# A four-layer graph network: layer 2's edge sums by bitwise and of two 8-bit adjacencies in place of matmuls in layer 1

## The chip, the cores and the metric

The kernel runs on one NeuronCore of a Trainium2 chip. The metric is the device time of one execution in microseconds (us); the number compared is the median of several runs. A profile is one further execution, recorded by the hardware profiler; its own time and the median of the other runs are not the same number, and both are given below.

## The reference, cut to what matters

There are N = 4096 nodes with D = 256 features, and one symmetric 0/1 adjacency `adj` (4096 x 4096, fp32) with ones on its diagonal. Four graph layers follow one another; each ends with `x = layernorm(x + layer(x, adj))`.

```python
# layer 0: mean over neighbours, concat, linear, relu
agg = adj @ x / max(deg, 1);  relu(concat([x, agg]) @ W + b)
# layer 1, two steps: R is adj + I with rows normed; A is a softmax attention cut to its top 0.9 of mass
A = top_p(softmax(q @ k.T));  Xf = R @ Xf;  Xa = A @ Xa;  Z += Xf @ U1.T + Xa @ U2.T
# layer 2, called with edge_features = adj
nn = adj @ x
ne = einsum('ij,ji->i', adj, edge_features)      # one number for each row
concat([x, nn, ne]) @ weight + bias
# layer 3: symmetric normed adjacency, linear, relu
```

The change is about `ne`: for row i it is the sum over j of `adj[i, j] * adj[j, i]`, a count of edges that exist both ways.

## The kernel before

**Tiling.** P = 128, so there are NT = 32 blocks of 128 rows. The host hands the adjacency over in two orders, both fp32 in DRAM: `adjt[it]`, the transposed blocks of block row `it` (a partition is a column, the layout that a matmul takes as its stationary side), and `adjn[it]`, the blocks of the other orientation. The main products run over a block row: 32 stationary tiles of 128x128 (fp32r, cast by ScalarE from 8-bit copies) against a moving 128x512 tile that holds the upper and the lower half of the features' bits side by side.

**Layer 0** (lines 220 to 349). `l0_main` loads `adjt[it]` in two halves by a DMA that casts fp32 to 8-bit (L276, on GpSimd's queue, 1 MB of source each) into a slot of the tag `in` (nine slots, eight of which first hold the input features), stores the 8-bit copy to `adj8_d[it]` in DRAM (L277, on SyncE's queue), and multiplies it. `column_counts` (L287) sums a block row's bits on VectorE: a tree of uint16 adds (L292, L294, L299), one shift (L296) and a cast (L301); one matmul with a column of ones (L306) ends the sum. The shift and the factor PER_ONE = 7 come from the bit pattern of an 8-bit 1.0. `l0_end` uses a layer norm whose reciprocal root is a GpSimd instruction (L197), and stores x1 and x1 + ln_b (L331, L332).

**Layer 1** (lines 352 to 1096) has two steps, n = 0 and 1. For each block i, `pieces` (L720) goes over eight chunks g of 512 columns; a chunk holds logits of block i+2 (L411), the attention product of block i, and `neighbours` (L674), which is R's product of block i+2 (acc_r, L683, with L685 for the identity). In step 0 the attention product is sparse: sixteen rows of x1 per node are fetched by indirect DMAs on GpSimd's queue (`gather`, L669, eight buffers; fetch k+8 follows the matmul of k) and multiplied by diagonal tiles (L758). In step 1 it is dense (turns L741, matmuls L766). VectorE finds the maxima and the kept ones (L430, L527, L660). `flag` (L579) counts by two fp32 matmuls (L589, L590) how many rows have to be put off to a later pass, and scatters their numbers (L603, GpSimd's queue).

In step 0 only, `neighbours` also makes `ne`: it loads `adjn[i]` in two halves by a casting DMA (L689, GpSimd's queue, into two slots of the step's pool) and multiplies each 8-bit tile of the one orientation by that of the other into one PSUM bank, tag `nef` (L693, 32 matmuls of 128x128 a block); `r_end` takes the diagonal of the result (L707) into column i of the tile `nef`. As `nef` is taken, acc_r has only the bank `acc` in step 0 (`r_acc`, L696, `nef_done`); later it has both in turn.

**Layers 2 and 3** (lines 1101 to 1184). `piece` loads a quarter of a block row of `adj8_d` (SyncE's queue, L1104, five slots) and casts it (ScalarE, L1106, four slots); `main` multiplies it. `l2_end` adds the residual and the parts (L1134, L1135 on VectorE, `nef` at L1137), and `l2_y` makes the operand of layer 3, for which layer 3 waits.

**What sets the order.** The kernel is written in a framework that builds all data dependencies and waits itself. It does not keep the program's order: at build time it plays the whole program against a list of costs, and gives each engine and each queue, at each moment, the earliest-written of the instructions whose data, buffers and engine are free. Each queue then runs in that fixed order on the chip; an instruction that waits holds up those behind it on its queue.

Names to keep: `ps_acc` is the PSUM pool with the two banks `acc` and `nef`; `half("mm")` and `half("acc")` are halves of two more banks; `hpool` holds the moving operand.

Of the kernel before, what the change touches and what calls it, by code (L numbers as in the profile page):

```python
# [24 lines left out]
P = 128  # L25
# [29 lines left out]
def gnn_stack(ctx, tc, x, adjt, adjn, w0, b0, w1, w2t, w3t, u1t, u2t, ln_g, ln_b, w2, b2, w3, b3, out):  # L55
# [44 lines left out]
    nc.vector.memset(ones_col, 1.0)  # L100
    mhalf = const.tile([P, 1], F32, name="mhalf")
# [18 lines left out]
    adj8_d = [dram.tile([P, NT, P], F8, name=f"adj8_{it}_d") for it in range(NT)]  # L120
    h_d = dram.tile([N + P, D], F32, name="h_d")
# [97 lines left out]

    with tc.tile_pool(name="l0", bufs=1) as l0, tc.tile_pool(name="l0w", bufs=2) as l0w:  # L220
# [28 lines left out]
        ones_bf = l0.tile([P, 1], BF16, name="ones_bf")  # L249
        nc.vector.memset(ones_bf, 1.0)  # L250
# [20 lines left out]
        def l0_main(it):  # L271
# [13 lines left out]
            return acc, column_counts(a8)  # L285

        def column_counts(a8):  # L287

            pairs = a8.bitcast(U16).rearrange("p j i -> p (j i)")
            W = NT * P // 4  # L290
            s = l0w.tile([P, W], U16, tag="sums", name="sums", bufs=1)
            nc.vector.tensor_add(s, pairs[:, :W], pairs[:, W:])  # L292
            W //= 2
            nc.vector.tensor_add(s[:, :W], s[:, :W], s[:, W : 2 * W])  # L294
            words = s[:, :W].bitcast(I32)
            nc.vector.tensor_scalar(words, words, 3, None, op0=ALU.logical_shift_right)  # L296
            while W > P // 2:
                W //= 2
                nc.vector.tensor_add(s[:, :W], s[:, :W], s[:, W : 2 * W])  # L299
            counts = l0w.tile([P, P], BF16, tag="counts", name="counts")  # L300
            nc.vector.tensor_copy(counts, s[:, :W].bitcast(U8))  # L301
            return counts
# [49 lines left out]
    with tc.tile_pool(name="l1", bufs=1, reuse_waits="tile") as l1:  # L352

        cur = {"late": False, "n": 0, "nef_done": False}
# [4 lines left out]
        ones_sq = l1.tile([P, P], F32, name="ones_sq")  # L359
        nc.vector.memset(ones_sq, 1.0)  # L360

        before = l1.tile([P, P], F32, name="before")
# [216 lines left out]
        def flag(st):  # L579
# [9 lines left out]
            nc.tensor.matmul(pb[:, 0:1], ones_sq, st["bad"], start=True, stop=True)  # L589
            nc.tensor.matmul(pb[:, 1:2], before, st["bad"], start=True, stop=True)  # L590
# [83 lines left out]
        def neighbours(n, i, g, acc_r, pn, xf):  # L674
# [11 lines left out]
            if pn is not None:  # L686
                if g % (NLC // 2) == 0:
                    cur["b8"] = cur["w"].tile([P, NT // 2, P], F8, tag="adjn8", name="adjn8", bufs=2)
                    nc.gpsimd.dma_start(cur["b8"], adjn[i, :, g * GP : g * GP + NT // 2, :])  # L689
                k = g % (NLC // 2) * GP  # L690
                for j in range(GP):
                    jt = g * GP + j
                    nc.tensor.matmul(pn[:, :P], cur["a8"][:, g % 2 * GP + j, :], cur["b8"][:, k + j, :], start=(jt == 0),  # L693
                                     stop=(jt == NT - 1))

        def r_acc(i):  # L696

            return ps_acc.tile([P, 512], F32, tag=("acc", "nef")[i % 2 if cur["nef_done"] else 0], name="acc_r", bufs=1)

        def r_end(i, acc_r, pn):  # L700
# [3 lines left out]
            if pn is not None:  # L704

                junk = spare_row.bitcast(F32)[:, :P]
                nc.vector.scalar_tensor_tensor(junk, pn[:, :P], 1.0, ident, op0=ALU.mult, op1=ALU.mult,  # L707
                                               accum_out=nef[:, i : i + 1])
            nc.sync.dma_start(rows(xf_d, i), xf_new)

        def r_product(n, i, xf):

            acc_r, pn = r_acc(i), None
            if n == 0:
                pn = ps_acc.tile([P, 512], F32, tag="nef", name="nef_ps", bufs=1)
            for g in range(NLC):
                neighbours(n, i, g, acc_r, pn, xf)
# [508 lines left out]
```

## Time and profile before

| | us |
|---|---|
| median of 3 runs | 3256.97 (3252.47 to 3258.52) |
| profiled execution, its own time | 3212.81 |
| its span, first to last instruction | 3211.1 |
| PE busy | 2949.0 (92%) |
| VectorE (DVE) busy | 2289.4 (71%) |
| ScalarE (ACT) busy | 1745.9 (54%) |
| GpSimd (POOL) busy | 786.8 (25%) |
| edge matmuls L693: first to last start | 359.9 to 1191.7 |
| R's product L683, both steps | 366.7 to 2468.1 |
| layer 2's matmuls | 2683.5 to 2960.8 |
| layer 3's matmuls | 2961.4 to 3197.1 |

How to read it: "busy" is the union of an engine's instructions. A busy PE is not PE at its peak, since matmuls are pipelined and each record reaches past the start of the next one: what a group of matmuls costs is read from its first start to the next group's start. The share of busy time is an average over stages with different limits; a stage has to be read from its own stretch. "DMA share" is the mean busy share of the core's sixteen DMA engines. A line such as "X L1 <- Y L2: total, times, longest" says that engine X sat idle before line L1 until line L2 on Y released it. PEld is the loading of stationary tiles, POOLq and SPq are the queues on which GpSimd and SyncE issue DMAs.

### The profile page before, as it was taken

What the parts mean: (1) busy time and instruction counts of PE and PEld (TensorE: products, weight loads), DVE (VectorE), ACT (ScalarE), POOL (GpSimd) and SP (SyncE); (2) the same over time, 40 slices, a digit from 0 to 9 for tenths busy, and PEclk for the clock granted to TensorE, in tenths of its full rate; (3) what the DMA queues carried; (4) which work ended last, traced back from release to release, by engine and by line L of the source; (5) the groups of instructions that cost most, each with busy time, mean ns of one, the idle gap of its engine ahead of it and who ended that gap; (6) DMA issues with size and microseconds to landing.
All of it is one profiled execution on the core that took longest, in us unless ns stands there. A gap on an engine that the chain in (4) does not pass through costs nothing. (4 is left out here: it accounts for less than half of the span.)

```text
span 3211.1 us, 45754 instructions
## 1 busy us (share of the span) xinstructions
PE 2949.0 (92%) x14376; PEld 2329.4 (73%) x14376; DVE 2289.4 (71%) x7161; ACT 1745.9 (54%) x2906; POOL 786.8 (25%) x915
## 2 busy tenths in 40 slices
PE   8999889999999996799989899989999796999998
PEld 3788667777777774578877777877788554887886
DVE  4666778888888875269979896988799664444444
ACT  3555655666666654365545454545555334666664
POOL 1121256677666763000000001000100100000000
PEclk9999999999999998899999999999999898999999
DMA  9995467777778774310001110111011234333332
GB/s 175 164 173 117 83 114 141 144 143 143 141 142 150 152 140 118 118 50 25 24 24 27 34 39 24 32 32 37 29 35 27 71 119 139 109 108 101 106 110 81
DMA packets 247872, 300.14 MB, mean 93 GB/s; under 512 B 34688, under 2 KB 201536, under 8 KB 247616
## 3 DMA queue, kind: packets, MB, share of 16 engines
q0 software_dynamic: 46576, 104.94, 22.9%
q1 hardware_dynamic: 188800, 180.93, 18.4%
q10 hardware_dynamic: 12240, 11.23, 1.1%
q8 instruction: 116, 1.90, 0.2%
q14 instruction: 140, 1.15, 0.2%
HBM read 331.17 MB, written 66.45 MB: 124 GB/s over the span
## 5 line engine op out<-in xcount | busy, mean ns | idle before, releaser
L683 PE MATMUL acc_r<-xh,adjq 128*128 128x512 f32 x2048 | 608.5, 428 | 27.7 <-ACT adjq L680 18.6
L766 PE MATMUL acc_bank<-xa,at 128*128 128x256 f32 x2304 | 565.6, 386 | 27.9 <-ACT at L744 27.3
L669 POOL DMA_INDIRECT G<-x_d,cols x512 | 496.1, 969 | 262.6 <-PE acc_bank L758 154.1
L680 ACT CAST adjq<-adj 128x512 fp32r<-128x512 fp8e4 x512 | 316.5, 620 | 386.5 <-PE acc_r L683 308.2
L766 PEld LDWEIGHTS acc_bank<-xa,at 128*128 128x128 f32 x2304 | 422.3, 193 | 88.2 <-ACT at L744 38.7
L683 PEld LDWEIGHTS acc_r<-xh,adjq 128*128 128x128 f32 x2048 | 376.0, 191 | 123.1 <-ACT adjq L680 45.4
L197 POOL TENSOR_TENSOR rstd<-ve,mhalf 128x1 f32<-128x1 f32 x168 | 103.1, 614 | 1337.8 <-DVE ve L195 1270.5
L430 DVE MAX8 cand<-e 128x8 f32<-128x256 f32 x1024 | 382.9, 415 | 65.0 <-ACT e L412 63.7
L412 ACT COPY e<-lg 128x512 f32<-128x512 f32 x552 | 319.5, 585 | 195.8 <-PE lg L411 191.9
L411 PE MATMUL lg<-kS,q 128*128 128x512 f32 x1104 | 398.2, 446 | 4.6 <-ACT e L412 4.5
L1106 ACT CAST a<-a 128x1024 fp32r<-128x1024 fp8e4 x256 | 267.9, 1048 | 156.7 <-PE acc L173 121.3
L758 PE MATMUL acc_bank<-G,dg 128*128 128x256 f32 x1024 | 288.5, 399 | 61.8 <-DMA G<-x_d,cols 48.2
L527 DVE FIND_INDEX8 cols<-top,e 128x8 uint32<-128x4096 f32 x64 | 282.8, 4419 | 0.0
L758 PEld LDWEIGHTS acc_bank<-G,dg 128*128 128x128 f32 x1024 | 195.1, 196 | 117.8 <-DMA G<-x_d,cols 65.9
L173 PE MATMUL acc<-xh,a 128*128 128x512 f32 x1024 | 255.0, 402 | 20.2 <-DMA a<-adj_d 15.5
L173 PE MATMUL acc<-y0h,a 128*128 128x512 f32 x1024 | 253.6, 401 | 0.0
L173 PEld LDWEIGHTS acc<-xh,a 128*128 128x128 f32 x1024 | 190.6, 189 | 63.8 <-ACT xh L149 23.0
L173 PE MATMUL acc<-yh,a 128*128 128x512 f32 x1024 | 233.7, 390 | 0.0
L744 ACT COPY at<-at_ps 128x512 f32<-128x512 f32 x296 | 173.5, 588 | 98.7 <-PE at_ps L741 97.0
L173 PEld LDWEIGHTS acc<-yh,a 128*128 128x128 f32 x1024 | 192.2, 188 | 39.6
L173 PEld LDWEIGHTS acc<-y0h,a 128*128 128x128 f32 x1024 | 188.1, 188 | 42.0 <-issue 0.6
L185 ACT COPY xt<-tr 128x256 f32<-128x256 f32 (+1 forms) x268 | 111.9, 425 | 189.8 <-PE tr L183 172.8
(287 smaller groups left out, 4588.0 us busy)
## 6 DMA issues: line engine op xcount, KB each, us to landing
adj<-adj_d SPq DMA_DIRECT2D x256, 128.0 KB
a<-adj_d SPq DMA_DIRECT2D x256, 128.0 KB
a<-in_adjt POOLq DMA_DIRECT2D x64, 256.0 KB
adj_d<-a SPq DMA_DIRECT2D x64, 256.0 KB
adjn<-in_adjn POOLq DMA_DIRECT2D x64, 256.0 KB
x_d<-x SPq DMA_DIRECT2D x64, 128.0 KB
xf_d<-xf_new SPq DMA_DIRECT2D x64, 128.0 KB
G<-x_d,cols POOLq DMA_INDIRECT x512
```

What stands on the lines that cost most here:

```text
L173: nc.tensor.matmul(acc, a[:, j, :], halves(jt), start=(jt == 0), stop=(jt == NT - 1))
L411: nc.tensor.matmul(pl[:, :LC], q[k], kS[:, s], start=(k == 0), stop=(k == 1))
L412: nc.scalar.copy(l[:, s], pl[:, :LC])
L430: nc.vector.max(dst[:, 8 * g : 8 * g + 8], src[:, g * GW : (g + 1) * GW])
L527: nc.vector.max_index(st["at"][:, 8 * r : 8 * r + 8], t8, st["e"][:, :N])
L669: nc.gpsimd.indirect_dma_start(out=g, out_offset=None, in_=x1_d, in_offset=bass.IndirectOffsetOnAxis(ap=st["at"][:, k : k + 1], axis=0))
L680: nc.scalar.copy(a, cur["a8"][:, g % 2 * GP : (g % 2 + 1) * GP, :])
L683: nc.tensor.matmul(acc_r, a[:, j, :], xf[:, jt, :], start=(jt == 0), stop=False)
L744: nc.scalar.copy(at[:, :G, :], ps[:, :G, :])
L758: nc.tensor.matmul(acc_a, dg[:, k % 4, :], st["G"][k], start=(k == 0), stop=(k == KEPT - 1))
L766: nc.tensor.matmul(acc_a, ats[g][:, j, :], cur["xa"][:, jt, :], start=(jt == 0), stop=(jt == NT - 1))
L1106: nc.scalar.copy(a, a8)
```

## The change

It makes a second 8-bit copy in DRAM, `adjn8_d`, by 64 DMAs that read `adjn` in fp32 and write 8 bits, written in the program at chunks 0 and 4 of each block of step 1. The edge matmuls, their loads and the diagonal leave step 0. In layer 2 each block loads its 512 KB row of `adjn8_d` (`edge_row`, two slots, SyncE's queue), VectorE takes the bitwise and with each of the four pieces (`both`), and `column_counts`, now with a pool as argument, sums the bits; `edge_count` ends the sum by a matmul and two small VectorE instructions. Beside that: acc_r uses both banks in step 0 too; `flag` casts `bad` to bf16 and takes bf16 matmuls; two adds of `l2_end` move to GpSimd; and the scratch of layer 2's first loads shares its slot with the second half of layer 3's operand.

```diff
@@ -98,6 +98,8 @@
     make_identity(nc, ident)
     ones_col = const.tile([P, 1], F32, name="ones_col")
     nc.vector.memset(ones_col, 1.0)
+    ones_bf = const.tile([P, 1], BF16, name="ones_bf")
+    nc.vector.memset(ones_bf, 1.0)
     mhalf = const.tile([P, 1], F32, name="mhalf")
     nc.vector.memset(mhalf, -0.5)
     rs = const.tile([P, NT], F32, name="rs")
@@ -118,6 +120,7 @@
     list_d = [dram.tile([N + P, 1], I32, name=f"list{n}_d") for n in range(STEPS)]
     adj8_d = [dram.tile([P, NT, P], F8, name=f"adj8_{it}_d") for it in range(NT)]
+    adjn8_d = [dram.tile([P, NT, P], F8, name=f"adjn8_{it}_d") for it in range(NT)]
     h_d = dram.tile([N + P, D], F32, name="h_d")
     k_d = dram.tile([N + P, P], F32, name="k_d")
@@ -215,6 +218,24 @@
         up = upper(ps[:, :P])
         nc.scalar.copy(dst[:DA, :], up[:DA, :])
         nc.vector.tensor_sub(dst[DA:, :], ps[DA:, :P], up[DA:, :])
+
+
+    def column_counts(pool, a8):
+
+        pairs = a8.bitcast(U16).rearrange("p j i -> p (j i)")
+        W = NT * P // 4
+        s = pool.tile([P, W], U16, tag="sums", name="sums", bufs=1)
+        nc.vector.tensor_add(s, pairs[:, :W], pairs[:, W:])
+        W //= 2
+        nc.vector.tensor_add(s[:, :W], s[:, :W], s[:, W : 2 * W])
+        words = s[:, :W].bitcast(I32)
+        nc.vector.tensor_scalar(words, words, 3, None, op0=ALU.logical_shift_right)
+        while W > P // 2:
+            W //= 2
+            nc.vector.tensor_add(s[:, :W], s[:, :W], s[:, W : 2 * W])
+        counts = pool.tile([P, P], BF16, tag="counts", name="counts", bufs=2)
+        nc.vector.tensor_copy(counts, s[:, :W].bitcast(U8))
+        return counts
     with tc.tile_pool(name="l0", bufs=1) as l0, tc.tile_pool(name="l0w", bufs=2) as l0w:
@@ -246,8 +267,6 @@
         x1 = xpool.tile([P, NT, D], F32, tag="X", name="x1")
         y0h = hpool.tile([P, NT, 2 * D], F32R, tag="H", name="y0h")
         deg1 = l0.tile([P, NT], F32, name="deg1")
-        ones_bf = l0.tile([P, 1], BF16, name="ones_bf")
-        nc.vector.memset(ones_bf, 1.0)
         def l0_weights(it, xt):
@@ -282,24 +301,7 @@
                 return a
             adj_matmul(l0w, acc, it, lambda jt: y0h[:, jt, :], piece)
-            return acc, column_counts(a8)
-
-        def column_counts(a8):
-
-            pairs = a8.bitcast(U16).rearrange("p j i -> p (j i)")
-            W = NT * P // 4
-            s = l0w.tile([P, W], U16, tag="sums", name="sums", bufs=1)
-            nc.vector.tensor_add(s, pairs[:, :W], pairs[:, W:])
-            W //= 2
-            nc.vector.tensor_add(s[:, :W], s[:, :W], s[:, W : 2 * W])
-            words = s[:, :W].bitcast(I32)
-            nc.vector.tensor_scalar(words, words, 3, None, op0=ALU.logical_shift_right)
-            while W > P // 2:
-                W //= 2
-                nc.vector.tensor_add(s[:, :W], s[:, :W], s[:, W : 2 * W])
-            counts = l0w.tile([P, P], BF16, tag="counts", name="counts")
-            nc.vector.tensor_copy(counts, s[:, :W].bitcast(U8))
-            return counts
+            return acc, column_counts(l0w, a8)
         def l0_degrees(it, counts):
             pd = half("acc")
@@ -351,15 +353,15 @@
     with tc.tile_pool(name="l1", bufs=1, reuse_waits="tile") as l1:
-        cur = {"late": False, "n": 0, "nef_done": False}
+        cur = {"late": False, "n": 0}
         FIRST = [[range(k * NT // 16, (k + 1) * NT // 16) for k in range(2)]]
         FIRST.append([range(5 * NT // 32, 8 * NT // 32), range(8 * NT // 32, 11 * NT // 32)])
-        ones_sq = l1.tile([P, P], F32, name="ones_sq")
+        ones_sq = l1.tile([P, P], BF16, name="ones_sq")
         nc.vector.memset(ones_sq, 1.0)
-        before = l1.tile([P, P], F32, name="before")
+        before = l1.tile([P, P], BF16, name="before")
         nc.gpsimd.affine_select(before, ones_sq, pattern=[[1, P]], compare_op=ALU.is_gt, fill=0.0, base=0,
                                 channel_multiplier=-1)
         ident_r = l1.tile([P, P], F32R, name="ident_r")
@@ -586,8 +588,10 @@
                 st["nb"] = small("nbad", 1, I32)[:1, :]
                 nc.scalar.copy(st["nb"], pb[:1, :1])
                 return
-            nc.tensor.matmul(pb[:, 0:1], ones_sq, st["bad"], start=True, stop=True)
-            nc.tensor.matmul(pb[:, 1:2], before, st["bad"], start=True, stop=True)
+            bad = small("bad16", 1, BF16)
+            nc.vector.tensor_copy(bad, st["bad"])
+            nc.tensor.matmul(pb[:, 0:1], ones_sq, bad, start=True, stop=True)
+            nc.tensor.matmul(pb[:, 1:2], before, bad, start=True, stop=True)
             sofar, slot = small("sofar"), small("slot")
             nc.vector.tensor_add(sofar, later["base"], pb[:, 0:1])
@@ -671,7 +675,7 @@
         GP = LC // P
-        def neighbours(n, i, g, acc_r, pn, xf):
+        def neighbours(n, i, g, acc_r, xf):
             if g % 2 == 0:
                 cur["a8"] = cur["w"].tile([P, 2 * GP, P], F8, tag="adj8", name="adj8", bufs=3)
@@ -683,39 +687,27 @@
                 nc.tensor.matmul(acc_r, a[:, j, :], xf[:, jt, :], start=(jt == 0), stop=False)
             if g + 1 == NLC:
                 nc.tensor.matmul(acc_r, ident_r, xf[:, i, :], start=False, stop=True)
-            if pn is not None:
-                if g % (NLC // 2) == 0:
-                    cur["b8"] = cur["w"].tile([P, NT // 2, P], F8, tag="adjn8", name="adjn8", bufs=2)
-                    nc.gpsimd.dma_start(cur["b8"], adjn[i, :, g * GP : g * GP + NT // 2, :])
-                k = g % (NLC // 2) * GP
-                for j in range(GP):
-                    jt = g * GP + j
-                    nc.tensor.matmul(pn[:, :P], cur["a8"][:, g % 2 * GP + j, :], cur["b8"][:, k + j, :], start=(jt == 0),
-                                     stop=(jt == NT - 1))
+        def second_copy(i, k):
+
+            half = slice(k * NT // 2, (k + 1) * NT // 2)
+            nc.gpsimd.dma_start(adjn8_d[i][:, half, :], adjn[i, :, half, :])
         def r_acc(i):
-            return ps_acc.tile([P, 512], F32, tag=("acc", "nef")[i % 2 if cur["nef_done"] else 0], name="acc_r", bufs=1)
-
-        def r_end(i, acc_r, pn):
+            return ps_acc.tile([P, 512], F32, tag=("acc", "nef")[i % 2], name="acc_r", bufs=1)
+
+        def r_end(i, acc_r):
             xf_new = work.tile([P, D], F32, tag="xf_new", name="xf_new", bufs=1)
             nc.scalar.activation(xf_new, acc_r[:, :D], AF.Copy, scale=rs[:, i : i + 1])
             nc.vector.scalar_tensor_tensor(xf_new, acc_r[:, D:], rs[:, i : i + 1], xf_new, op0=ALU.mult, op1=ALU.add)
-            if pn is not None:
-
-                junk = spare_row.bitcast(F32)[:, :P]
-                nc.vector.scalar_tensor_tensor(junk, pn[:, :P], 1.0, ident, op0=ALU.mult, op1=ALU.mult,
-                                               accum_out=nef[:, i : i + 1])
             nc.sync.dma_start(rows(xf_d, i), xf_new)
         def r_product(n, i, xf):
-            acc_r, pn = r_acc(i), None
-            if n == 0:
-                pn = ps_acc.tile([P, 512], F32, tag="nef", name="nef_ps", bufs=1)
+            acc_r = r_acc(i)
             for g in range(NLC):
-                neighbours(n, i, g, acc_r, pn, xf)
-            r_end(i, acc_r, pn)
+                neighbours(n, i, g, acc_r, xf)
+            r_end(i, acc_r)
         def pieces(n, st, nxt, ops, rs_now=()):
@@ -730,9 +722,7 @@
             with_r = st is not None and len(rs_now) > 0
             if with_r:
                 i, = rs_now
-                acc_r, pn = r_acc(i), None
-                if n == 0:
-                    pn = ps_acc.tile([P, 512], F32, tag="nef", name="nef_ps", bufs=1)
+                acc_r = r_acc(i)
             ats = {}
             def turn(g):
@@ -766,7 +756,7 @@
                         nc.tensor.matmul(acc_a, ats[g][:, j, :], cur["xa"][:, jt, :], start=(jt == 0),
                                          stop=(jt == NT - 1))
                 if with_r:
-                    neighbours(n, i, g, acc_r, pn, cur["xf"])
+                    neighbours(n, i, g, acc_r, cur["xf"])
                 for f in ops.get(g, ()):
                     f()
             if st is None:
@@ -779,7 +769,7 @@
                     put(xa_d, st, xa_new)
                 st["xa"] = xa_new
             if with_r:
-                r_end(i, acc_r, pn)
+                r_end(i, acc_r)
         def put(dst, st, t):
@@ -1006,6 +996,9 @@
                 if cd is not None:
                     peak_groups(cd)
                     at(1, exp_rows, cd)
+                if n and i >= 0:
+                    at(0, second_copy, i, 0)
+                    at(4, second_copy, i, 1)
                 for job in jobs:
                     at(1, advance, job)
                 if cd is not None:
@@ -1046,7 +1039,6 @@
                 cur["late"] = True
                 fetch(n, jobs[0]["st"])
                 cur["late"] = False
-                cur["nef_done"] = True
                 for i in range(FIRST[1][0][0]):
                     r_product(1, i, cur["next"])
             todo = []
@@ -1099,28 +1091,50 @@
     with tc.tile_pool(name="l23", bufs=1, reuse_waits="tile") as l23:
-        def piece(it, c):
+        def piece(it, c, edges=False):
             a8 = l23.tile([P, JP, P], F8, tag="a8", name="a8", bufs=5)
             nc.sync.dma_start(a8, adj8_d[it][:, c * JP : (c + 1) * JP, :])
+            if edges:
+                both(it, c, a8)
             a = l23.tile([P, JP, P], F32R, tag="adjt", name="a", bufs=4)
             nc.scalar.copy(a, a8)
             return a
-        ahead = [piece(0, c) for c in range(NJP)]
-        zh = load_halves(l23.tile([P, 4 * J0 * D], F32, name="scratch"), zu_d[:N, :], nc.sync, slice(0, D))
+        def edge_row(it):
+
+            b8 = l23.tile([P, NT, P], F8, tag="b8", name="b8", bufs=2)
+            nc.sync.dma_start(b8, adjn8_d[it])
+            return b8
+
+        def both(it, c, a8):
+
+            b = edge_rows[it][:, c * JP : (c + 1) * JP, :].bitcast(I32)
+            nc.vector.tensor_tensor(b, b, a8.bitcast(I32), op=ALU.bitwise_and)
+
+        def edge_count(it):
+
+            counts = column_counts(l23, edge_rows.pop(it))
+            ps = half("acc")
+            nc.tensor.matmul(ps[:, 0:1], counts, ones_bf, start=True, stop=True)
+            n = l23.tile([P, 1], I32, tag="edges", name="edges", bufs=2)
+            nc.vector.tensor_scalar(n, ps[:, 0:1], 1.0 / PER_ONE, None, op0=ALU.mult)
+            nc.vector.tensor_copy(nef[:, it : it + 1], n)
+
+        edge_rows = {0: edge_row(0), 1: edge_row(1)}
+        ahead = [piece(0, c, True) for c in range(NJP)]
+        zh = load_halves(l23.tile([P, NT * D], F32, tag="X", name="scratch"), zu_d[:N, :], nc.sync, slice(0, D))
+        yh = [pool.tile([P, NT // 2, 2 * D], F32R, tag="X", name=f"yh{k}") for k, pool in enumerate((xpool, l23))]
         w2e_sb = load_bcast(l23, w2[2 * D, :], "w2e_sb")
         b2_sb = load_bcast(l23, b2, "b2_sb")
         w3_sb = load_w(l23, w3, "w3_sb")
         b3_sb = load_bcast(l23, b3, "b3_sb")
-        yh = [pool.tile([P, NT // 2, 2 * D], F32R, tag="X", name=f"yh{k}") for k, pool in enumerate((xpool, l23))]
-
         def y_halves(jt):
             return yh[2 * jt // NT][:, jt % (NT // 2), :]
-        def main(it, halves):
+        def main(it, halves, edges=False):
             acc = ps_acc.tile([P, 512], F32, tag=("acc", "nef")[it % 2], name="acc")
-            adj_matmul(l23, acc, it, halves, lambda it, c: ahead.pop(0) if ahead else piece(it, c))
+            adj_matmul(l23, acc, it, halves, lambda it, c: ahead.pop(0) if ahead else piece(it, c, edges))
             return acc
         def l2_end(it, acc):
@@ -1131,8 +1145,8 @@
             nc.sync.dma_start(xi, rows(x2_d, it))
             u = l23.tile([P, D], F32, tag="u", name="u", bufs=2)
             nc.sync.dma_start(u, rows(zu_d, it)[:, D:])
-            nc.vector.tensor_add(xi, xi, b2_sb)
-            nc.vector.tensor_add(u, u, xi)
+            nc.gpsimd.tensor_add(xi, xi, b2_sb)
+            nc.gpsimd.tensor_add(u, u, xi)
             t = l23.tile([P, D], F32, tag="t", name="t", bufs=2)
             nc.vector.scalar_tensor_tensor(t, w2e_sb, nef[:, it : it + 1], nn, op0=ALU.mult, op1=ALU.add)
             nc.vector.tensor_add(t, t, u)
@@ -1168,7 +1182,10 @@
         done = []
         for it in range(NT):
-            acc = main(it, lambda jt: zh[:, jt, :])
+            acc = main(it, lambda jt: zh[:, jt, :], True)
+            edge_count(it)
+            if it + 2 < NT:
+                edge_rows[it + 2] = edge_row(it + 2)
             if it > 1:
                 l2_y(it - 2, done.pop(0))
             if it > 0:
```

## The prediction

> **What bounds the kernel now.** I read the stretches first (busy time of each engine in stretches that I chose by the first and last start of each stage's matmuls), then the groups by line, the waits, and the timelines of PE, POOL and SP.
>
> ```profile
> core 0: us, PE busy (x) PEld busy (x) DVE busy (x) ACT busy (x) POOL busy (x), PEclk, DMA share, GB/s
> 0.00:50.00 50.00, 34.18 (x91) 16.50 (x92) 20.76 (x66) 15.22 (x37) 6.39 (x17) 0.97 1.00 198
> 50.00:265.00 215.00, 215.00 (x949) 161.46 (x947) 133.74 (x521) 112.50 (x161) 40.18 (x74) 1.00 1.02 164
> 265.00:345.00 80.00, 80.00 (x380) 64.65 (x379) 49.51 (x200) 42.26 (x55) 6.56 (x12) 1.00 0.29 79
> 407.00:1190.00 783.00, 735.67 (x4071) 582.80 (x4070) 643.07 (x1933) 472.56 (x912) 533.12 (x564) 0.98 0.76 142
> 1400.00:2450.00 1050.00, 983.00 (x4951) 811.78 (x4952) 899.93 (x2987) 560.17 (x938) 81.61 (x101) 0.98 0.12 31
> 2710.00:2961.00 251.00, 251.00 (x1120) 202.21 (x1119) 108.33 (x324) 162.05 (x234) 16.45 (x30) 1.00 0.34 110
> ```
>
> Rows 1 to 3 are layer 0, then step 0, step 1, and layer 2. PE leads everywhere, but with different runners-up: in layer 0 the DMA engines are full (1.00 and 1.02) up to 265 us and nearly idle (0.29) for the last 80; in step 0 DVE (82%), POOL (68%) and DMA (0.76) are all high; in step 1 DMA and POOL are nearly empty; in layer 2 PE never pauses and DVE is at 43%.
>
> In step 0 the waits and the PE timeline say what holds PE up:
>
> ```profile
> PEld acc_bank L758 <- DMA G<-x_d,cols: 57.0, 45, 8.2
> ```
> ```profile
> 800.33 0.40 PE L693 MATMUL nef_ps<-adjn,adj 128*128 128x128 fp8e4 x4
> 800.53 0.70 PE L411 MATMUL lg<-kS,q 128*128 128x512 f32 x2
> ...
> 829.57 0.70 PE L758 MATMUL acc_bank<-G,dg 128*128 128x256 f32 x2 [1.14 <-DMA G<-x_d,cols]
> ```
>
> Four edge matmuls hold PE for 0.20 us (start to next start), and PE also waits some 57 us in the stage for gathered rows G. The matmuls of acc_r (L683), which could fill those waits, don't: the next block's first ones start at 807.16, after r_end has emptied the one bank.
>
> The third thing to see is the order on the queues:
>
> ```profile
> L802 SPq DMA_DIRECT2D x<-x1b_d x1: 320/320/320, 103.2 to 103.2; - x1
> ```
> ```profile
> 1.59 1.34 POOL L276 DMA_DIRECT2D a<-in_adjt  x2
> 23.04 1.06 POOL L276 DMA_DIRECT2D a<-in_adjt  x2 [20.12 <-PE tr L183]
> ```
>
> L802 fetches x1b only in step 1 (fetch skips it for n = 0). Its first instance is issued at 103.2 us, in layer 0, 3.4 us after that row was stored (L332 at 99.77), and some 1200 us before step 1. So the program's place does not hold a DMA back: it goes as soon as its data and buffer are there and its queue is idle. And POOL's queue is idle for 20 us near the start, because the layer-0 loads wait for slots.
>
> [...]
>
> **The second copy (added, moved).** 64 casting DMAs of 1 MB source now write DRAM in place of SBUF tiles. Before, L689's loads could not go ahead: they needed an SBUF slot of step 0 (two). The new ones read an input and write a fresh DRAM tensor: no data, no slot. By the reading of L802 I expect them on POOL's queue in the first idle gap of layer 0, ahead of most of L276's loads, not in step 1. There the DMA engines are full. Price of one: the hardware queues moved 180.93 + 11.23 MB in 18.4% + 1.1% of the span, 626 us, so 3.26 us a MB. Layer 0's plain DMAs are 64 stores of 256 KB, 8 of 512 KB, and 96 of 128 KB: 33.6 MB, 109 us. Its DMA time is 50 + 215 + 0.29 x 80 = 288 us; the rest, 179 us over 64 casting loads, is 2.8 us each. With a write to DRAM it may be up to 0.85 us more (256 KB at 3.26). I take 3.0: 64 x 3.0 = 192 us, less the 57 us that the engines have free after 265: **layer 0 grows by 135 us** (122 at 2.8, 180 at 3.7). PE has nothing to do meanwhile: the mains of later blocks need loads that are queued behind. POOL's own time (0.6 us each, L689) is hidden in its idle gaps; what is queued behind on POOL are L276's loads and rstd (L197), for which DVE's layer norm waits.
>
> **Step 0 (removed).** Per block: 8 groups of edge matmuls, 8 x 0.20 = 1.6 us of PE; two POOL issues of 0.6 + 0.3; DVE's L707, 0.35; 2 casting DMAs (5.6 us of the engines); and acc_r now has two banks, so its matmuls can stand in the waits for G. The block takes 783/30 = 26.1 us. Floors afterwards: PE from 825.49 to 852.25 is 26.8 less 2.4 of waits for G = 24.4, less 1.6 and 0.2 (flags) = 22.6; POOL 16 x 1.25 (gather start to start) + 1.66 (list_d) = 21.7; DVE 643/30 = 21.4 less 0.2. Three engines near 22 in one ring (flag, list, gathers, matmul, logits, flag) do not reach the floor: I take 24.0, so 2.1 x 30 = 63, and with the products ahead of the first block **65 us less**. Ends: 20 (PE's gain turned into longer waits for G) and 105 (the floor).
>
> **Flags, both steps.** Four fp32 passes (816.79 to 817.21, 0.42 us) become two bf16 ones; the counts matmul of layer 0 (L306, 0.17 us) is the nearest row, so some 0.2 us less PE a block. Against it, a 128x1 copy (0.14 us, L558) stands between bad and the flags, for which PE waits in step 1. Step 0's share is in its floor; step 1: 32 x (0.2 - 0.1) = **3 us less** (10 less to 6 more).
>
> **Layer 2 (added).** DVE per block: 108.33/251 of 8.53 us = 3.7; plus 4 bitwise ands at 0.42 = 1.7; the count chain at layer 0's rows, 0.69 + 0.41 + 0.29 + 0.28 + 0.22 + 0.19 + 0.22 = 2.3; two small ones 0.3; less the two adds moved to POOL, 0.85. Sum 7.1, plus the 0.73 of waiting for rstd: 7.9 of PE's 8.53. So PE still leads, with 0.1 us more for the edge matmul. The adds on POOL have no row; [...] at the low end 32 x 0.1 = 3. I take 0.3 a block, 10 us. The first two edge rows, 1 MB ahead of layer 2's first pieces, cost 3.3 us. **13 us more.** Waits added: the edge matmul on PE waits for DVE's counts, with the next block's matmuls behind it; SP's load of row it+2 waits for the counts that read the slot, with the next pieces behind it. The four pieces already cast (4 x 2.1 us) cover both.
>
> **Sum.** 135 - 65 - 3 + 13 = 80 us more. The profiled execution took 3212.8 us (span 3211.1, 1.7 around it): 3293. The median of the runs is 44 us above it, 3257; I add the same 80: **3337**.
>
> **Rivals.**
> 1. *The copies are issued in step 1, in the program's order* (faster). For it: POOL is busy 82 of 1050 us there and the DMA engines 0.12, so the 192 us of transfers would lie beside other work. Against it: L802 at 103.2, and x0i (L325), which is issued at 14.3 us and read near 95. Step 1 then costs perhaps 3: -65 - 3 + 13 + 3 = -52, 3205. It decides if fewer than some 19 + 17 of the 64 copies land in layer 0: 57 us of free DMA takes 19, and each further one costs 3.0 against the 52 gained.
> 2. *They are spread*: half in layer 0 (96 - 57 = 39), the rest in step 0, where POOL and DMA then keep their load. -52 + 39 = -13, 3244.
> 3. *Layer 2 becomes DVE's*: 35 more on top of the forecast, 3372. [...] against it: the cover above.
>
> **Chances.** Copies in layer 0: 0.66 (rival 3 is its upper part, 0.15 of that). Spread: 0.12. In step 1: 0.22. The likeliest case's own range, from the ends of its four terms taken together, is 3290 to 3405. The range must reach into rival 1, whose own spread is 40 us either way: 3195 to 3405 leaves out about 0.08 on each side. A difference of 0.2% is about what a measurement of this kernel can tell from none: faster 0.28 (rival 1 and half of 2), the same 0.03, slower 0.69.
>
> **What would show it.** The first start of the copy's DMA on POOL's queue: in layer 0 (right) or after 1240 us (rival 1). The last layer-0 matmul near 480 us, not 345, with the DMA share at 1.0 up to there and PE waiting for a<-in_adjt. Step 0's block near 24 us, with L683 inside the old waits for G. Layer 2's block near 8.8 us, PE still leading; over 9.2 says rival 3. If POOL's first gap holds no copy, the forecast is wrong as a whole.

## The result, and the profile after

In four runs each on one chip, the changed kernel took 3376.64 us (3374.15 to 3383.17) and the kernel before 3257.74 us (3252.47 to 3265.11): ratio 1.0364, 95% interval 1.0341 to 1.0387. The forecast was 3337 in a range of 3195 to 3405: the sign and the main cause hold, the size is 40 us short, and one term of the sum is wrong. The same program, run again in another sitting ("paced", below), was 1.3% slower than the before beside it, not 3.6%.

The stretches of the changed kernel, as shown of before (us; busy time and count of each engine; granted clock; DMA share; GB/s). Rows 1 to 4 are layer 0, then step 0, step 1, layer 2:

```profile
core 0: us, PE busy (x) PEld busy (x) DVE busy (x) ACT busy (x) POOL busy (x), PEclk, DMA share, GB/s
0.00:50.00 50.00, 25.35 (x60) 12.31 (x61) 12.60 (x43) 11.78 (x27) 8.89 (x22) 0.93 1.03 183
50.00:265.00 215.00, 88.06 (x290) 54.24 (x289) 48.78 (x160) 33.48 (x65) 42.78 (x81) 0.69 1.05 130
265.00:410.00 145.00, 145.00 (x696) 118.30 (x696) 93.50 (x386) 81.85 (x106) 29.34 (x54) 1.00 1.03 174
410.00:490.00 80.00, 79.76 (x383) 64.93 (x382) 49.31 (x204) 42.77 (x57) 5.79 (x12) 1.00 0.29 74
545.00:1360.00 815.00, 700.08 (x3072) 556.15 (x3071) 636.19 (x1901) 462.75 (x910) 492.75 (x505) 0.94 0.51 117
1560.00:2610.00 1050.00, 995.18 (x5064) 819.00 (x5063) 931.39 (x3144) 583.33 (x974) 84.72 (x104) 0.99 0.12 32
2862.00:3130.00 268.00, 262.61 (x1173) 204.34 (x1172) 192.98 (x638) 161.84 (x243) 60.56 (x85) 1.00 0.49 153
```

In layer 0 the DMA engines are full (share 1.03 to 1.05) up to 410 us instead of 265, and the 80 us tail at a share of 0.29 is still there. In the second row PE works 88 of 215 us. The copies' line says why:

```profile
L693 POOL DMA_DIRECT2D adjn_d<-in_adjn x64: 517/517/767, 1.6 to 220.3; - x64
...
who waited for it (us, times):
  POOL adjn_d L693: 75.2, 37
  POOL a L295: 18.0, 8
```

All 64 copies are issued between 1.6 and 220.3 us, none in step 1. The last layer-0 load goes out at 409.6 us, where it went out at 265.5. What POOL's queue looks like at its first idle gap (start, duration, what ended the idle time):

```profile
1.58 2.86 POOL L693 DMA_DIRECT2D adjn_d<-in_adjn  x5
4.43 1.11 POOL L295 DMA_DIRECT2D a<-in_adjt  x2
30.66 1.06 POOL L295 DMA_DIRECT2D a<-in_adjt  x2 [25.12 <-PE tr L186]
31.70 3.09 POOL L693 DMA_DIRECT2D adjn_d<-in_adjn  x6
```

Stages, read from the first and last starts of their matmuls (us). G are the gathered rows of step 0. "Before again" and "paced" are runs told of below; paced has the changed kernel's instructions in the changed kernel's order:

| | before | before again | after | paced |
|---|---|---|---|---|
| layer 0 ends at | 345.7 | 350.9 | 488.7 | 489.0 |
| step 0, to the last product with G | 909.3 | 973.3 | 937.7 | 823.5 |
| to the first dense product of step 1 | 149.3 | 149.6 | 154.4 | 152.6 |
| step 1, first to last dense product | 1250.0 | 1256.6 | 1211.1 | 1219.2 |
| to layer 2 | 29.2 | 31.5 | 32.7 | 32.7 |
| layer 2 | 277.3 | 277.4 | 293.5 | 296.3 |
| layer 3 | 236.3 | 236.3 | 240.3 | 240.3 |

So the loss is layer 0's. Step 0, from which the forecast took 65 us, gave nothing against the first profile of before, and the table already shows why that comparison is unsafe: one kernel's step 0 is 909 in one execution and 973 in another.

### The profile page after: what moved, and what is told of

Same layout as the page of the kernel before. It is cut to its first block, busy times and chain, and to the rows that moved or that the text cites. A ratio compares the mean times of both kernels' runs of the same rounds, so it can differ in the third digit from the quotient of the medians.

```text
span 3372.5 us, 43851 instructions
## 1 busy us (share of the span) xinstructions
PE 2904.0 (86%) x13256; PEld 2283.1 (68%) x13256; DVE 2376.6 (70%) x7513; ACT 1732.7 (51%) x2906; POOL 832.5 (25%) x979
## 5 line engine op out<-in xcount | busy, mean ns | idle before, releaser
L687 PE MATMUL acc_r<-xh,adjq 128*128 128x512 f32 x2048 | 618.5, 432 | 49.4 <-ACT adjq L684 26.8
L687 PEld LDWEIGHTS acc_r<-xh,adjq 128*128 128x128 f32 x2048 | 384.0, 195 | 152.9 <-ACT adjq L684 56.9
L1100 ACT CAST a<-a 128x1024 fp32r<-128x1024 fp8e4 x256 | 263.4, 1047 | 115.2 <-PE acc L176 77.8
L748 PE MATMUL acc_bank<-G,dg 128*128 128x256 f32 x1024 | 281.1, 400 | 32.9 <-DMA G<-x_d,cols 17.2
L176 PE MATMUL acc<-xh,a 128*128 128x512 f32 x1024 | 262.3, 408 | 25.7 <-DVE xh L153 23.3
L413 PEld LDWEIGHTS lg<-kS,q 128*128 128x128 f32 x1104 | 195.8, 194 | 63.7 <-ACT e L414 22.7
L300 ACT CAST a<-a 128x1024 fp32r<-128x1024 fp8e4 x128 | 132.2, 1046 | 194.0 <-DVE bn L194 74.8
```

What stands on the lines that cost most here:

```text
L176: nc.tensor.matmul(acc, a[:, j, :], halves(jt), start=(jt == 0), stop=(jt == NT - 1))
L413: nc.tensor.matmul(pl[:, :LC], q[k], kS[:, s], start=(k == 0), stop=(k == 1))
L687: nc.tensor.matmul(acc_r, a[:, j, :], xf[:, jt, :], start=(jt == 0), stop=False)
L748: nc.tensor.matmul(acc_a, dg[:, k % 4, :], st["G"][k], start=(k == 0), stop=(k == KEPT - 1))
L1100: nc.scalar.copy(a, a8)
```

## The experiments

Line numbers shift by one or two from kernel to kernel; names tell the groups.

**Copies held in step 1.** Each pair of copies is queued behind the list's scatter of its block.

```diff
+            cur["scatter"] = nc.gpsimd.indirect_dma_start(out=list_d[...], ...)
...
-            nc.gpsimd.dma_start(adjn8_d[i][:, half, :], adjn[i, :, half, :])
+            with tc.issue_after(cur["scatter"].ins):
+                nc.gpsimd.dma_start(adjn8_d[i][:, half, :], adjn[i, :, half, :])
```

> The changed kernel, with each copy's DMA put behind the list scatter of step 1 on GpSimd's queue, so that no copy is issued before step 1. Theory (the copies sit in layer 0 on GpSimd's queue): layer 0's last matmul goes back from 489 to about 346 us, step 1 grows by 0 to 10, in all 3376 - 143 + 5 = about 3238 us. Rival (the place of the copies does not matter; step 0's new order and layer 2 on VectorE cost the time): 3350 or more.

3354.81 us (3345.61 to 3362.41), ratio 1.0246 (1.0207 to 1.0284). Layer 0 ends at 343.8 us again: the copies in layer 0 made the 143 us. But step 1 takes 1317.5 us, 82 more than without copies (next run), where a few were expected. ACT's casts wait for the 8-bit loads; here, then in the kernel without copies, over the same stage (total, times, longest):

```profile
PEld acc_bank L757 <- ACT at L735: 87.4, 33, 12.0
...
ACT adjq L684 <- DMA adj<-adj_d: 71.8, 9, 11.3
```
```profile
PEld acc_bank L756 <- ACT at L734: 44.8, 34, 7.4
...
ACT adjq L684 <- DMA adj<-adj_d: 29.0, 7, 5.5
```

With two copies in flight the longest wait for a 128 KB load is 11.3 us, not 5.5. Behind that cast on ACT's queue stand the copies `at`, for which PE waits 43 us more (87.4 against 44.8), about half of the 82. The DMA share in this stage was 0.41.

**No second copy.** Layer 2 reads the first 8-bit adjacency twice.

```diff
-                    at(0, second_copy, i, 0)
-                    at(4, second_copy, i, 1)
...
-            nc.sync.dma_start(b8, adjn8_d[it])
+            nc.sync.dma_start(b8, adj8_d[it])
```

> The changed kernel without the second copy: layer 2 reads the first 8-bit copy twice in its place (this input's adjacency is symmetric, so the sums are the same numbers; for another input they would not be). Theory: as with the copies held back, less what they cost step 1: 3225 to 3240 us. Rival: 3350 or more.

3265.01 us (3249.1 to 3275.12), ratio 0.996 (0.9945 to 0.9976). Everything but the copies comes out 0.4% ahead (11 us), not 55 us. Layer 2 takes 297.5 us, step 1 1235.8, step 0 947.7.

**rstd off GpSimd in layer 0.** With the copies in layer 0, the waits of the changed kernel there are headed by

```profile
DVE x L205 <- POOL rstd L200: 111.3, 13, 103.1
POOL adjn_d L693 <- DMA adjn_d<-in_adjn: 75.2, 37, 2.6
ACT a L300 <- DVE bn L194: 74.8, 1, 74.8
```

One rstd waited 103 us behind copies that wait for earlier copies. Is that the loss?

```diff
-        nc.gpsimd.tensor_tensor(r, ve, mhalf, op=ALU.pow)
+        nc.scalar.activation(r, ve, AF.Sqrt)
+        nc.vector.reciprocal(r, r)
```

> The changed kernel, copies in layer 0 as they are, but layer 0's reciprocal root of the layer norm made by ScalarE (root) and VectorE (reciprocal) in place of GpSimd. If layer 0 is long because the layer norm waits on GpSimd's queue behind the copies, PE's matmuls no longer stop between about 130 and 225 us, layer 0 ends near 425 us (DMA engines full to about 410, then the last blocks) and the whole takes about 3376 - 64 = 3312 us. If it is long because the DMA engines are full, layer 0 still ends near 489 and the whole takes 3370 to 3385.

3403.27 us (3401.81 to 3405.27), ratio 1.0402 (1.0371 to 1.0434); layer 0 ends at 492.2 us. That wait alone isn't the loss. Another takes its place:

```profile
ACT a L304 <- DMA adj_d<-a: 106.1, 4, 72.9
PEld acc L176 <- ACT a L304: 93.4, 2, 68.6
```

On ACT's queue the casts stand behind the issue of x0i, which waits for a store of the 8-bit adjacency. The stores are late with their loads: SyncE waits 329 us for those in this run, 205 us in before.

**The kernel before without edge sums.** Loads, matmuls and diagonal are left out, and nef is a constant.

```diff
-            if pn is not None:
+            if False:
...
+    nc.vector.memset(nef, 33.0)
```

> The kernel before without the edge matmuls, their loads and the diagonal: the edge sums are left out (a constant stands in their place). Theory of the prediction (PE, GpSimd and the gathers all get room): 1.6 us or more a block, 3257 - 55 = about 3202 us, down to 3180. Rival (step 0 is a ring of waits through GpSimd's gathers, VectorE and ScalarE, in which PE's gain turns into waits): 3240 to 3257.

3287.14 us (3279.09 to 3300.28), ratio 1.0037 (1.0022 to 1.0053): nothing gained; step 0 takes 981.2 us. The work that the forecast took out of step 0 was not what set its length, in this execution at least; the next run shows how far that goes.

**The kernel before again.** The same code, one profile.

> The kernel before, profiled once more, because its first profiled execution lay 44 us under the median of its runs. Own theory: the 44 us lie in step 0, which then lasts some 940 us from the end of layer 0 to the last product with gathered rows (909 in the first profile), so that the changed kernel's step 0 (938) is neither a gain nor a loss. Rival: step 0 is again near 909, and the change made it some 30 us longer.

3291.35 us, where runs of before on that chip had a median of 3282.14. Step 0 took 973.3 us, 64 more than in the first profile, and the other stages agree within 7. So of the 79 us between the two profiles 64 are step 0's. That the 44 us between the first profile and the median of before lie there too is likely, but those runs were not profiled.

**16-bit or fp32 flags.** The kernel without copies, the flags put back.

```diff
-        ones_sq = l1.tile([P, P], BF16, name="ones_sq")
+        ones_sq = l1.tile([P, P], F32, name="ones_sq")
...
```

> The changed kernel without the second copy (layer 2 reads the first 8-bit adjacency twice, which is valid for this symmetric adjacency), and the put-off counts with fp32 operands as before. Forecast: the flags are worth 3 us a step, so 3271 where the same kernel with 16-bit operands had 3265. Rival: the 14 to 39 us by which step 1 became shorter are the flags', since PE waits for them there; then step 1 is back at 1250 and the whole at 3280 to 3300.

3300.3 us, ratio 1.0053 (1.0037 to 1.0069). Against the next run on the same chip, which has 16-bit flags and differs in one PSUM bank besides (ratio 0.9989), that is 21 us; step 1 is 1253.3 against 1236.9. The two profiles differ by 10 us in all, as step 0 is 16 us shorter in this one.

**One bank for acc_r in step 0.**

```diff
-            return ps_acc.tile(..., tag=("acc", "nef")[i % 2], ...)
+            return ps_acc.tile(..., tag=("acc", "nef")[i % 2 if cur["n"] else 0], ...)
```

> The changed kernel without the second copy, with one PSUM bank for acc_r in step 0, as before. Forecast's theory: the second bank lets the products stand in the waits for G and was worth some 20 to 30 us; without it 3285 to 3295, and PE's waits for G are back above 40 us. Own theory now: a ring of waits over DVE, POOL and the DMA engines sets step 0, and the bank is worth nothing: 3260 to 3270, step 0 at 948.

3278.78 us (3267.09 to 3306.45), ratio 0.9989 (0.9975 to 1.0003), step 0 984.7 us. The ratio is 0.3% over that of the kernel with two banks, measured on another chip: some 10 us. Step 0 of the profile is 37 us longer than there, but this execution was the second slowest of 22. By the medians the bank is not worth the 20 to 30 us that the forecast's theory asks for; with the chips apart this is not a sharp test.

**Matmuls without use in step 0.** As the last, with 32 matmuls of 128 columns a block.

```diff
+                    nc.tensor.matmul(cur["pad"][:, :P], e8, e8, start=(jt == 0), stop=(jt == NT - 1))
```

> As the kernel with one bank and no second copy, with 32 matmuls of 128 columns a block put back in step 0, where the edge matmuls stood; their result is not used, and no loads and no sums come with them. Forecast's theory (PE's work sets step 0): 51 us more than without them. Theory of the ring: nothing, within 5 us. Theory of the clock (PE's gaps lower the granted clock, and the matmuls left run slower): PE busier, its clock in step 0 back from 0.94 to 0.97 or more, and the time equal or 10 to 30 us less.

3272.39 us (3263.1 to 3287.9), ratio 0.9982 (0.996 to 1.0004): 1024 matmuls more, no time more. Step 0 without and with them:

```profile
405.00:1250.00 845.00, 698.54 (x3015) 556.73 (x3014) 626.68 (x1861) 457.78 (x900) 489.85 (x498) 0.92 0.51 111
```
```profile
407.00:1240.00 833.00, 743.52 (x3961) 580.03 (x3960) 638.22 (x1889) 467.48 (x905) 496.02 (x503) 0.95 0.55 114
```

PE's share goes from 83% to 89% and its clock from 0.92 to 0.95. The ring's theory allows that; the clock's asked for 0.97 or more, which did not come. The forecast's theory, that PE's work sets step 0 (51 us more), falls for executions like these.

**16-bit flags alone, in the kernel before.**

> The kernel before with one part of the change alone: the put-off counts with 16-bit operands (ones_sq, before and a 16-bit copy of bad). Forecast's figure: 3 us less a step, within 0.2% of before. Own theory from the pair of kernels without the copy (16-bit 1236 us, fp32 1253 us between the first and the last product of step 1): some 17 to 21 us less, ratio 0.993 to 0.995, step 1 near 1235.

3226.81 us (3207.0 to 3232.73), ratio 0.9936 (0.9912 to 0.996): the flags are worth 0.6% alone, as in the pair above. This version beats both kernels. Its step 1, 1243.4 us, is only 7 under the first profile of before, and 13 under before again, so the place of the rest isn't shown.

**Copies held in step 0.** As the first experiment, with `n == 0`.

> The changed kernel with the 64 copies held behind the list's scatter as in the run that held them in step 1, but in step 0, where they stand in for the loads that the change removed. Theory that step 0 waits in a ring and has DMA time to spare (share 0.51, the loads of before had raised it to 0.76 at no cost): no loss against the kernel without copies, ratio 0.996 to 1.000, step 0 near 950, DMA share near 0.7. Rival, that a copy costs what it cost in step 1 (82 to 106 us), because it holds up whatever waits for a DMA: step 0 at 1030 to 1060, ratio 1.02 to 1.03.

3339.82 us (3334.47 to 3346.05), ratio 1.0292 (1.0269 to 1.0316): the rival's ratio came. Step 0 takes 1015.6 us, a little under the rival's 1030, 68 more than in the kernel without copies (another chip) and 192 more than in the next run, taken beside it. PE waits for G, 187.6 us in 893, where the next run has 70.2 in 735:

```profile
PE acc_bank L749 <- DMA G<-x_d,cols: 149.5, 33, 9.3
...
PEld acc_bank L749 <- DMA G<-x_d,cols: 38.1, 15, 6.2
```

POOL's timeline of one block:

```profile
703.27 1.16 POOL L694 DMA_DIRECT2D adjn_d<-in_adjn  x2
705.50 1.03 POOL L673 DMA_INDIRECT G<-x_d,cols  x1 [1.06 <-PE acc_bank L749]
...
715.55 0.94 POOL L673 DMA_INDIRECT G<-x_d,cols  x1 [2.73 <-DMA adjn_d<-in_adjn]
718.70 0.95 POOL L673 DMA_INDIRECT G<-x_d,cols  x1 [2.21 <-DMA G<-x_d,cols]
```

The gathers stand behind two copies on one queue. Before with 16-bit flags, run beside it, had as many casting loads here and the edge matmuls too, and its step 0 took 917.1 us; its loads came one half row at a time (two a block, some 12.6 us apart). Whether the pairing or the write to DRAM makes the copies dearer was not tested.

**Copies paced in step 1.** Each copy was to follow a matmul of its own chunk.

```diff
+                        cur["mm"] = nc.tensor.matmul(acc_a, ats[g][:, j, :], ...)
...
+            with tc.issue_after(cur["mm"].ins):
```

> The changed kernel with each copy of step 1 held behind a matmul of its own block (the two halves of a row four chunks apart), not both behind one scatter. Theory that the burst of two copies holds up the loads of a<-adj_d on which the products wait: step 1's extra falls from 82-106 us to under 40, ratio 1.000 to 1.010. Rival, that the copies' bytes cost the same however spread, or that POOL's queue (list scatter, rstd) waits behind them: step 1 stays at 1300 or more, ratio 1.02 or more.

The edit did not do what it says. The matmul is on PE, the copies are on POOL's queue, and they went out from 1.6 to 219.9 us as before. In the built programs this kernel and the changed one have the same instructions in the same order on every engine and queue, line numbers apart: the run is a repeat of the changed kernel. It took 3283.86 us (3269.31 to 3298.44), ratio 1.0131 (1.0105 to 1.0156), against 1.0364. Layer 0 is the same to 0.3 us; step 0 is 823.5 us instead of 937.7. So pacing was not tested, and something else came out.

**Edge rows cast into SBUF in layer 2.** No copy; layer 2 loads from the fp32 adjacency.

```diff
-            nc.sync.dma_start(b8, adjn8_d[it])
+            for k in range(2):
+                half_row = slice(k * NT // 2, (k + 1) * NT // 2)
+                nc.gpsimd.dma_start(b8[:, half_row, :], adjn[it, :, half_row, :])
```

> The changed kernel without the second copy: layer 2 loads its edge rows straight from the fp32 adjacency with casting loads on GpSimd's queue (two of 1 MB a block, 2.3 to 3.0 us each of the 16 DMA engines). Layer 2's DMA work is 0.51 x 297 us less some 50 us for the 8-bit rows, plus 64 x 2.3 to 3.0 us: 250 to 290 us. Own theory: it just fits, layer 2 takes 300 to 320 us and the whole is 5 to 25 us above the kernel without a copy; ratio 1.000 to 1.005 where step 0 takes about 948 us, as in most runs, and 0.96 to 0.98 where it takes some 825, as it did with the same order of instructions in the run called paced. Rival: the DMA engines or GpSimd's queue (rstd behind loads that wait for a buffer) set layer 2, which then takes 340 us or more.

3404.51 us (3385.38 to 3410.65), ratio 1.0371 (1.035 to 1.0392). Layer 2 takes 402.6 us, 105 more than without a copy: my theory fell, the rival's number came, at another place. The DMA share is 0.67, not full. The largest new wait for a DMA is DVE's, for the small 8-bit pieces; in this kernel (340 us of it) and then in the changed one (268 us):

```profile
DVE b L1111 <- DMA a<-adj_d: 141.0, 56, 6.7
```
```profile
DVE b L1112 <- DMA a<-adj_d: 47.7, 43, 1.7
```

## Why the forecast was right in sign and short in size

**Layer 0: right, by two errors that cancel.** 135 us were forecast, 143 came, and holding the copies back removes them; that the number is so near is luck. The place (first idle gap of POOL's queue, none in step 1) is as told. The working was 64 x 3.0 less 57 us of free DMA time. Measured, the time at full share grew by 145 us (410 against 265), 2.3 us a copy; and the 57 us were not used at all, since the copies go ahead of the loads and the tail is PE's work after the last load. Whether a load, once issued, also stood behind copies issued before it, no run separates: the runs show that the loads were issued later (the last at 409.6 us, not 265.5). The sign to look for, PE waiting for a<-in_adjt, wasn't there: PE waited for casts that stood behind rstd and behind x0i's issue. From 265 us on PE pauses for 0.24 us only, so whether full DMA engines or PE's late start set the end is not separated; the run without rstd on POOL shows that one of these waits alone isn't it.

**Step 0, "65 us less": the step that failed.** It rested on one profile in which PE was at 94% and waited 57 us for G. The profiles of step 0 fall in two groups, called rhythms here, and that profile had the short one:

- Short: the first profile of before (909 us), before with 16-bit flags (917) and paced (823), the last two on one chip in one sitting. There edges and bank together are worth 94 us, near the far end of 105. A block takes 23.8 us on the mean from scatter to scatter in paced, 26.8 in before with 16-bit flags; 26.1 and 24.0 were forecast. Some blocks come near POOL's floor of 21.7, as this one of paced with 22.4:

```profile
1158.25 0.99 POOL L607 DMA_INDIRECT list_d<-ids,slots  x1 [0.31 <-issue]
...
1180.63 0.99 POOL L607 DMA_INDIRECT list_d<-ids,slots  x1 [0.30 <-issue]
```

- Long: before again (973), before without edges (981), without copies (948 to 985), after (938; 27.5 a block). There PE's work can be taken out or put back without effect: two edits did it, both at nothing. Between before again and after, step 0 differs by 36 us; what gives these is not shown.

The four runs of before that stand beside the changed kernel were not profiled, so which rhythm they had isn't known. If before again stands for them, its stages and those of after differ by 138 - 36 + 5 - 45 + 1 + 16 + 4 = 83 us, about the forecast; the medians differ by 119. In the other sitting the profiles of paced and of before with 16-bit flags differ by 43 us; the medians of these two differ by 57, since the profile of paced was the fastest of its six runs. The forecast's own profile had the short rhythm, while the median of before was 44 us longer. If the runs of the result had the long rhythm, as the profile of after did, then "I add the same 80" carried a saving of one rhythm into the other.

What picks the rhythm stays open. It isn't the kernel: one program had both. Nor is it the chip: the short sitting and the one with before again used the same one, and before took 3243.49 us in one, 3282.14 in the other. As far as seen it goes by sitting: the three profiles of the short one are not long, and those of the three other sittings on record all are. What grows is mostly waiting, not work. Step 0 in after, then in paced, from first to last product with G:

```profile
545.00:1426.00 881.00, 736.87 (x3195) 582.08 (x3194) 670.64 (x1979) 480.90 (x939) 525.38 (x537) 0.92 0.52 119
```
```profile
545.00:1312.00 767.00, 692.61 (x3188) 560.40 (x3187) 667.16 (x1979) 478.67 (x937) 521.84 (x537) 0.96 0.63 136
```

DVE, ACT and POOL are busy for the same time in both; PE is busy 44 us more of the 114, at a lower clock (last section).

The profiles of the long rhythm also have, in step 0, waits that end at an event which the profile puts to no instruction (it calls them "remote"); there are none in the four that are not long (the fourth is that of the copies held in step 0):

```profile
POOL G L673 <- remote: 42.9, 27, 4.1
```

This one is of the kernel with one bank. Counting the events in the traces shows that they are missing from the record, not late. In step 0 paced has 13021 landings for its 816 DMAs (35 short of 16 each) and 3360 of 3369 events of PE, DVE and ACT; after, with the same instructions, has 4172 and 2124. All ten long profiles are like after, the four others like paced, and outside step 0 all have 98% or more. So a wait in step 0 read from a long profile must not be set beside one from a short profile; starts and busy times can be. Whether the lost events and the longer time have one cause, no run separates.

**Flags, "3 us less": mis-sized.** 21 us over the kernel in the first pair and 0.6% again in the second; in step 1, for which 3 were forecast and 10 at most, 16 in the first pair and 7 against the first profile of before. The forecast counted PE's time; more was gained than that, and where is not settled.

**Layer 2, "13 us more": right.** 16 us and 3.5 ahead of it. PE leads with 262.61 of 268 us, so the third rival (3372, by a DVE bound) is wrong; that its number lies near the result is chance. Its 35 us, and the 0.3 us a block that the forecast took for the adds on GpSimd, were the author's estimates, which no row of before shows. Measured, those adds took 0.83 and 0.77 us. The 0.42 us of a bitwise and was that of a DVE add of before (L1135, 420 ns); measured, it is 0.43 (L1112, 432 ns). DVE waits 47.7 us for a<-adj_d, which no step foresaw, at little cost.

**Rival 1's price.** Kept in step 1, the copies were to cost 3 us, as the share of 0.12 left room. They cost 82, and with them held there the kernel was 79 us slower than the before beside it, where this rival said 52 faster: 131 us wrong.

## What to carry to other kernels

Ask of a DMA that depends on nothing where its queue is first idle: the 64 copies, written in step 1, went out there, from 1.6 to 220.3 us, and what stood behind them on that queue waited (one rstd for 103 us). A low DMA share was no room for 1 MB casting DMAs: held in step 1 (share 0.12), put in step 0 (0.51) or in layer 2, their stage grew by 68 to 105 us against the kernel without copies (in step 0 by 192 against the run beside it), and each time small loads or gathers that something waits for came late. And before a term is taken from one profile, see whether a second profile of the same kernel has that stage at the same length.

## What the runs showed of the hardware that I had not expected

PE ran slow after a pause. In step 0 of after, then of paced, the same eight matmuls:

```profile
1238.08 0.59 PE L748 MATMUL acc_bank<-G,dg 128*128 128x256 f32 x2
1240.62 3.68 PE L809 MATMUL mm_bank<-u,xt 128*128 128x256 f32 x8 [1.95 <-issue]
1244.13 0.60 PE L748 MATMUL acc_bank<-G,dg 128*128 128x256 f32 x2
```
```profile
1167.72 0.67 PE L749 MATMUL acc_bank<-G,dg 128*128 128x256 f32 x2 [0.50 <-DVE cand L531]
1168.22 1.89 PE L810 MATMUL mm_bank<-u,xt 128*128 128x256 f32 x8
1169.95 0.59 PE L749 MATMUL acc_bank<-G,dg 128*128 128x256 f32 x2
```

From start to next start (the records reach 0.17 and 0.16 us past it) they take 3.51 us after a pause of 1.95 and 1.73 us after one of 0.50. The granted clock (third number from the end) of after just before the pause and over the slow matmuls:

```profile
1230.00:1238.00 8.00, 7.52 (x35) 5.71 (x34) 7.12 (x16) 6.68 (x15) 6.17 (x7) 1.00 0.64 73
1240.60:1244.10 3.50, 3.48 (x8) 2.77 (x9) 3.50 (x2) 2.92 (x6) 0.94 (x1) 0.52 0.52 157
```

The trace has it at 0.5 for 3.41 us and at 1.0 from 1244.13 on. Over step 0 of the fourteen profiles, the group of matmuls that follows a pause of more than 2.5 us lasts 1.6 to 2.0 times the shortest time of such a group, on the mean of each profile; one that follows no pause lasts 1.1 times. After a pause of 1 to 2.5 us it is not sure: 11 of 27 in after were followed by the half clock. In all, step 0 of after has 136.5 us at half clock and that of paced 61.4; by an estimate from these two (half of the difference) that is some 38 of the 114 us between them. With less work on PE the clock was lower too: in step 0 it was 0.96 in before again and 0.91 in before without edges, both of the long rhythm, so part of the work taken out came back as time at the lower clock.
